# An attention and recurrence kernel on one core: the start of the first batch reordered, and the residual adds of the recurrence put back into its steps

## The chip, the core and the metric

The kernel runs on one core of a Trainium2 chip. The metric is the time of one execution on the device in microseconds (us). A run is the median of several executions; the profile is that of one execution, and times inside it are counted from the start of its span. The engines are PE (TensorE's products; PEld is its weight load), DVE (VectorE), ACT (ScalarE), POOL (GpSimd) and SP (SyncE, which here only issues transfers).

## What is computed

The input x has the shape 4 x 128 x 64 x 64: four batches of 128 channels by 4096 positions. All is in 32-bit floats. Cut to what matters, the reference is:

```python
# layer 0
x = x + conv_attention(groupnorm(x, 32 groups))      # q, k: 64 x 128 weights, v: 128 x 128
                                                     # softmax over all 4096 positions
# layer 1, on tokens t = x transposed to (4, 4096, 128)
t = t + causal_attention(layernorm(t), Wq, Wk, Wv)   # scale 128 ** -0.5
t = t + ffn(layernorm(t), W, V, gamma, beta)
# the ffn
Wx = batchnorm(einsum('bti,hi->bth', t, W)) * gamma + beta   # over all batches and tokens
y = 0
for each token: y = sigmoid(Wx[token] + y @ V.T)             # 4096 steps, every y is an output
```

## The kernel before

**Storage.** `X` (128 partitions x 4 batches x 4096) stays in SBUF from the first load to the end. It is loaded by eight DMAs of 1 MB on SP's queue (L88 to L91). The weights and biases come by 17 DMAs on ACT's queue (L95, L104 to L107), W0k and W0q twice each, since q and k of 64 channels are laid on both halves of the partitions.

**Order of the work.** A scheduler sets the order of the instructions on each engine by the order in which the program makes them and by what they need; `keep_in_program_order` holds an instruction at its place in the program. The program itself lists units: a tile is (layer, batch, c) with 512 queries, a unit is two blocks of 128 keys. The loop at L496 makes the scores of unit i + 1 (L428), lets up to two queued jobs take a step (`turn`, L225), and then makes the product of unit i (L457). ACT takes the exponential of the scores with a shift (L441), DVE adds the exponentials up for the softmax's sums (L475). A job is a Python generator, such as `groupnorm`, `feed0` (keys and values of 512 positions), `prep0` (queries), `norm1` (layernorm), `end` (division by the sums) or `wx` (the ffn's first product); `complete` runs one to its end on the spot.

**Start of a batch.** `groupnorm` takes bn_stats of X in eight pieces (L260), aggregates them to mv (L264), takes the means of a group by a product (pg L267, copied to gmv L269), the spread of the means by another (dev L271 and L272, pd L275), the inverse root on DVE and POOL (L154, L155), scales the three weights by it (wk, wv, wq, L284), and folds the means into the biases (pb L288, L293). For batch 0 nothing else is there to be done meanwhile; `start_batch(0)` and `score(0)` (L494, L495) run all of it, then the keys and values of eight columns (pk L308, pv L313), the queries of the first tile (pq L319), and a sample of scores (`sample`, pz L238, maximum L242, pm L245, L247, px L250) from which the exponential's shift comes (L252). For layer 1 the product of Wq and Wk is made once ahead of everything (`wt`, pa, A1; L207 to L216); it needs W1q and W1k. `groupnorm` of batches 1 to 3 is queued by `start_batch` in layer 1 of the batch before (L480).

**The recurrence** (`chunks`, L518). The 4096 steps of a batch are cut into 256 chunks of 16 steps that run side by side; each chunk is warmed up by 12 steps of the chunk before. So there are 28 steps, s = -12 to 15, of four batches each: a product with FV on PE (pg L552, 128 x 256), then L554 on DVE (gain times Wx, added to it in PSUM), then the sigmoid on ACT (L555). From s = 0 on each result is added to the layer's input T, which was written to D in DRAM by L379 and loaded back by L193. For batches 0 and 1 POOL adds it in each step (L558, with a stride of 16 in T). For batches 2 and 3 the results are kept in `later`, and DVE adds them behind the last step in eight adds of 128 x 1024 (L567). `out` leaves by DMAs of 2 MB for batches 0 and 1 (L561) and of 1 MB for the other two (L573).

**The flag.** Behind the adds DVE compares the warm-up's last state with the neighbouring chunk's (d L578, L580, L581) and looks at the range of the softmax's sums with two reductions of 128 x 1024 (L587, L588). A product adds the verdicts up (pb L591) into a flag (L594); all engines load it and branch (L603, L604). With these inputs it is zero, and the slower second version, `whole`, is jumped over.

Of the kernel before, what the change touches and what calls it, by code (L numbers as in the profile page):

```python
# [37 lines left out]
L = 16  # L38
M = 4096 // L
LEAD = 12  # L40
# [24 lines left out]
def fast(  # L65
# [10 lines left out]
    nc = tc.nc  # L76
    B, C, N = x.shape
    CQ = w0q.shape[1]
    NQ = N // QT
# [4 lines left out]
    const = ctx.enter_context(tc.tile_pool(name="const", bufs=1))  # L84
    xpool = ctx.enter_context(tc.tile_pool(name="xres", bufs=1))

    X = xpool.tile([P, B, N], F32, name="X")
    for b in range(B):  # L88
        for h in range(2):
            cols = ts(h, N // 2)  # L90
            nc.sync.dma_start(out=X[:, b, cols], in_=x[b, :, cols])  # L91

    def load(src, shape, name):
        t = const.tile(shape, F32, name=name)
        nc.scalar.dma_start(out=t, in_=src)  # L95
        return t


    W0q = const.tile([P, 2, CQ], F32, name="W0q")
    W0k = const.tile([P, 2, CQ], F32, name="W0k")  # L100
    B0q = const.tile([P, 1], F32, name="B0q")
    B0k = const.tile([P, 1], F32, name="B0k")
    for h in range(2):
        nc.scalar.dma_start(out=W0k[:, h, :], in_=w0k)  # L104
        nc.scalar.dma_start(out=W0q[:, h, :], in_=w0q)
        nc.scalar.dma_start(out=B0k[ds(h * CQ, CQ), :], in_=b0k)
        nc.scalar.dma_start(out=B0q[ds(h * CQ, CQ), :], in_=b0q)  # L107
    W0v = load(w0v, [P, C], "W0v")
# [7 lines left out]
    Fbeta = load(fbeta, [P, 1], "Fbeta")  # L116


    ident = const.tile([P, P], F32, name="ident")
# [3 lines left out]
    ones = const.tile([P, P], F32, name="ones")  # L123
    nc.gpsimd.memset(ones, 1.0)
# [23 lines left out]
    gain = const.tile([P, 1], F32, name="gain")  # L148
# [46 lines left out]
    with ExitStack() as actx:  # L195
# [11 lines left out]
        wt = {}  # L207
        for n, w in (("q", W1q), ("k", W1k)):
            pw = ps_m.tile([P, P], F32, tag="m", name=f"pw_{n}")
            nc.tensor.transpose(pw, w, ident)  # L210
            wt[n] = tmp.tile([P, P], F32, tag="wt", name=f"wt_{n}")
            nc.vector.tensor_copy(wt[n], pw)
        pa = ps_m.tile([P, P], F32, tag="m", name="pa")
        nc.tensor.matmul(pa, lhsT=wt["q"], rhs=wt["k"], start=True, stop=True)
        A1 = const.tile([P, P], F32, name="A1")
        nc.vector.tensor_scalar(A1, pa, float(C) ** -0.5, None, ALU.mult)  # L216

        jobs = deque()

# [36 lines left out]
        def groupnorm(b):  # L256

            stats = small.tile([P, NQ, 6], F32, tag="stats", name=f"stats_{b}")
            for c in range(NQ):
                nc.vector.bn_stats(stats[:, c, :], X[:, b, ts(c, QT)])  # L260
                if c % 2:
                    yield
            mv = small.tile([P, 2], F32, tag="mv", name=f"mv_{b}")
# [6 lines left out]
            dev = small.tile([P, 1], F32, tag="dev", name=f"dev_{b}")  # L270
            nc.vector.tensor_tensor(dev, mv[:, 0:1], gmv[:, 0:1], ALU.subtract)  # L271
            nc.vector.tensor_tensor(dev, dev, dev, ALU.mult)  # L272
            yield
            pd = ps_m.tile([P, 1], F32, tag="m", name=f"pd_{b}")
            nc.tensor.matmul(pd, lhsT=gmat, rhs=dev, start=True, stop=True)  # L275
            nc.vector.tensor_tensor(gmv[:, 1:2], pd, gmv[:, 1:2], ALU.add)
            grs = small.tile([P, 1], F32, tag="grs", name=f"grs_{b}")
            rsqrt(grs, gmv[:, 1:2], 1e-5, 1)
            yield
            got = {}  # L280
            for n, w in (("k", W0k), ("v", W0v), ("q", W0q)):
                src = w if n == "v" else w.rearrange("p h o -> p (h o)")
                got[n] = small.tile([P, P], F32, tag=f"w{n}", name=f"w{n}_{b}")
                nc.vector.tensor_scalar(got[n], src, grs, None, ALU.mult)  # L284
# [123 lines left out]
        def score(i):  # L408
# [16 lines left out]
            ps = ps_pair.tile([P, 2, QT], F32, tag="pair", name=f"ps_{i}")  # L425
            for h in range(2):
                rows = slice(0, P) if layer else ds(h * CQ, CQ)
                nc.tensor.matmul(  # L428
                    ps[:, h, first[h] :], lhsT=K[layer, b][rows, ts(2 * u + h, P)],
                    rhs=Q[t][rows, first[h] :], start=True, stop=True,  # L430
                )
            if layer and u >= 2 * c:
# [85 lines left out]
def chunks(tc, X, T, gain, bias, FV, ones, sums, out, flag):  # L518
# [4 lines left out]
    with ExitStack() as ctx:  # L523
        yp = ctx.enter_context(tc.tile_pool(name="ys", bufs=5))
        keep = ctx.enter_context(tc.tile_pool(name="keep", bufs=1))
        ps_g = ctx.enter_context(tc.tile_pool(name="ps_g", bufs=1, space=PSUM))


        half = B // 2
        later = keep.tile([P, B - half, L, M], F32, name="later")  # L530
        WX = X.rearrange("p b (c s m) -> p b c s m", s=L, c=X.shape[2] // QT)

        lead = keep.tile([P, B, M + 1], F32, name="lead")
        nc.vector.memset(lead[:, :, 0:1], 0.0)
        last = None
        for s in range(-LEAD, L):
            if s == -1:
                Y = [lead[:, b, 1:] for b in range(B)]
            else:
                y = yp.tile([P, half if s >= 0 else B, M], F32, tag="Y", name=f"Y_{s + LEAD}")  # L540
                Y = [
                    later[:, b - half, s, :] if s >= 0 and b >= half else y[:, b, :] for b in range(B)
                ]
            for b in range(B):
                wx = WX[:, b, :, s % L, :]
                if last is None:
                    nc.scalar.activation(  # L547
                        Y[b].rearrange("p (c m) -> p c m", c=wx.shape[1]), wx, AF.Sigmoid, bias=bias, scale=gain
                    )
                    continue  # L550
                ps = ps_g.tile([P, M], F32, tag=f"g{b}", name=f"pg_{s + LEAD}_{b}")
                nc.tensor.matmul(ps, lhsT=FV, rhs=last[b], start=True, stop=True)  # L552
                pv = ps.rearrange("p (c m) -> p c m", c=wx.shape[1])
                nc.vector.scalar_tensor_tensor(pv, wx, gain, pv, ALU.mult, ALU.add)  # L554
                nc.scalar.activation(Y[b], ps, AF.Sigmoid, bias=bias)  # L555
                if s >= 0 and b < half:
                    t = T[b].rearrange("p (m s) -> p s m", s=L)[:, s, :]
                    nc.gpsimd.tensor_tensor(t, t, Y[b], ALU.add)  # L558
            last = [lead[:, b, :M] for b in range(B)] if s == -1 else Y
        for b in range(half):  # L560
            nc.sync.dma_start(out=out[b], in_=T[b])  # L561
        for b in range(half, B):
            t = T[b].rearrange("p (m s) -> p s m", s=L)
            for i in range(4):
                cols = ts(i, M // 4)
                tc.keep_in_program_order(
                    nc.vector.tensor_tensor(  # L567
                        t[:, :, cols], t[:, :, cols], later[:, b - half, :, cols], ALU.add
                    )
                )  # L570
                if i % 2:
                    cols = ts(i // 2, M * L // 2)
                    nc.sync.dma_start(out=out[b][:, cols], in_=T[b][:, cols])  # L573
        good = keep.tile([P, 4], F32, name="good")
        d = keep.tile([P, B, M - 1], F32, name="d")
        for b in range(B):
            tc.keep_in_program_order(
                nc.vector.tensor_tensor(d[:, b, :], lead[:, b, 1:M], last[b][:, : M - 1], ALU.subtract)  # L578
            )
# [490 lines left out]
```

## Time and profile before

| | |
|---|---|
| median of 5 runs | 2673.69 us (2672.82 to 2675.09) |
| the profiled execution | 2675.83 us |
| its span | 2674.3 us, mean granted clock 0.99 |
| DMA | 35.81 MB: HBM read 17.30 MB, written 16.78 MB |

The profile of this execution lists: the busy time of each engine; the span in slices, with the clock that PE was granted; the DMA queues; the chain of waits that ended last, followed back from the last instruction; the costliest groups of instructions; and the DMA issues with their time to landing. The trace behind it gives the same for any stretch of time or line. The stages are seen in these moments: the first load is issued at 0.80, the first exponential starts at 49.99, the last tile of attention ends its products at about 2571, the first sigmoid of the recurrence starts at 2593.02, the step s = 0 at 2616.30, the last step ends at about 2645.5, the last of `out` lands at 2666.89.

### The profile page before, as it was taken

What the parts mean: (1) busy time and instruction counts of PE and PEld (TensorE: products, weight loads), DVE (VectorE), ACT (ScalarE), POOL (GpSimd) and SP (SyncE); (2) the same over time, 40 slices, a digit from 0 to 9 for tenths busy, and PEclk for the clock granted to TensorE, in tenths of its full rate; (3) what the DMA queues carried; (4) which work ended last, traced back from release to release, by engine and by line L of the source; (5) the groups of instructions that cost most, each with busy time, mean ns of one, the idle gap of its engine ahead of it and who ended that gap; (6) DMA issues with size and microseconds to landing.
All of it is one profiled execution on the core that took longest, in us unless ns stands there. A gap on an engine that the chain in (4) does not pass through costs nothing.

```text
span 2674.3 us, 25646 instructions
## 1 busy us (share of the span) xinstructions
PE 2598.0 (97%) x9970; PEld 1223.4 (46%) x9970; DVE 1498.7 (56%) x2543; ACT 1118.9 (42%) x1302; POOL 100.2 (4%) x118
## 2 busy tenths in 40 slices
PE   6999999999999999999999999999999999999975
PEld 3444444445444444454444444444544444444443
DVE  4565556544555556554455555654455565655448
ACT  2444443333444444343444444333344444433345
POOL 0000000000000000000000000000000000000004
PEclk9999999999999999999999999999999999999988
DMA  3000000000000000000000000000000000100013
GB/s 134 1 1 1 1 0 11 9 5 4 5 1 1 1 1 5 12 4 5 8 1 1 1 1 1 8 12 4 5 4 1 1 1 1 67 13 4 8 67 127
DMA packets 9522, 35.81 MB, mean 13 GB/s; under 512 B 2224, under 2 KB 2992, under 8 KB 7088
## 3 DMA queue, kind: packets, MB, share of 16 engines
q1 hardware_dynamic: 7200, 33.56, 3.2%
q8 instruction: 80, 1.31, 0.2%
q10 hardware_dynamic: 2192, 0.53, 0.1%
q14 instruction: 50, 0.41, 0.1%
HBM read 17.30 MB, written 16.78 MB: 13 GB/s over the span
## 4 chain that ended last, share of the span: by engine, by line
PE 91%; DVE 6%; ACT 1%; issue 1%; DMA 1%; POOL 0%; ACTq 0%; DVEq 0%; POOLq 0%
PE av L457 47%; PE ps L428 32%; PE pg L552 2%; DVE tot L475 2%; PE pq L319 1%; ACT s L441 1%; PE pv L313 1%; PE pk L308 1%; PE po L377 1%; PE pq L340 1%; PE pw L389 1%; DVE zt L354 1%; DVE tot L351 1%; DVE part L356 1%; PE pt L161 1%
## 5 line engine op out<-in xcount | busy, mean ns | idle before, releaser
L457 PE MATMUL av<-s,V 64*128 64x512 f32 (+3 forms) x4864 | 1361.4, 587 | 0.0
L441 ACT ACTIVATE s<-ps,shift 128x1024 f32<-128x1024 f32 (+4 forms) x796 | 809.2, 1024 | 1317.5 <-PE ps L428 1177.3
L475 DVE TENSOR_TENSOR tot<-tot,s 128x1024 f32<-128x1024 f32 (+4 forms) x796 | 878.8, 1109 | 857.4 <-ACT s L441 732.9
L428 PE MATMUL ps<-q,K 64*128 64x512 f32 (+4 forms) x3200 | 1030.3, 579 | 0.0
L457 PEld LDWEIGHTS av<-s,V 64*128 64x128 f32 (+1 forms) x4864 | 546.0, 187 | 593.4 <-issue 585.9
L428 PEld LDWEIGHTS ps<-q,K 64*128 64x128 f32 (+1 forms) x3200 | 416.5, 188 | 483.4 <-issue 472.1
L457 PE MATMUL av<-tot,V 64*128 64x512 f32 (+2 forms) x384 | 124.6, 612 | 5.8 <-DVE acc L469 5.8
L441 ACT ACTIVATE tot<-ps,shift 128x1024 f32<-128x1024 f32 (+2 forms) x68 | 71.5, 1058 | 104.7 <-PE ps L428 84.0
L155 POOL TENSOR_TENSOR rstd<-rstd,mhalf 128x4 f32<-128x4 f32 x32 | 32.3, 1008 | 1443.8 <-DVE rstd L154 1443.8
L457 PEld LDWEIGHTS av<-tot,V 64*128 64x128 f32 (+1 forms) x384 | 49.5, 190 | 70.5 <-issue 39.1
L155 POOL TENSOR_TENSOR rstd_f<-rstd_f,mhalf 128x4 f32<-128x4 f32 x32 | 33.5, 1046 | 914.4 <-DVE rstd_f L154 914.4
L435 DVE TENSOR_TENSOR ps<-ps,mask 128x128 f32<-128x128 f32 x128 | 38.0, 297 | 33.8 <-PE ps L428 31.5
L174 DVE TENSOR_SCALAR V<-xt,mv,rstd 128x128 f32<-128x128 f32 x128 | 36.0, 342 | 34.5 <-POOL rstd L155 34.5
L174 DVE TENSOR_SCALAR rows<-xt_f,mv_f,rstd_f 128x128 f32<-128x128 f32 x128 | 36.7, 342 | 31.2 <-POOL rstd_f L155 31.2
L554 DVE SCALAR_TENSOR_TENSOR pg<-X,gain,pg 128x256 f32<-128x256 f32 x108 | 48.4, 489 | 5.4 <-PE pg L552 4.7
L354 DVE STREAM_TRANSPOSE zt<-tot 128x512 f32<-128x512 f32 x64 | 45.5, 710 | 2.1
L378 DVE TENSOR_TENSOR X<-X,po 128x512 f32<-128x512 f32 x32 | 22.0, 687 | 43.8 <-PE po L377 43.8
L351 DVE TENSOR_TENSOR tot<-tot 128x512 f32<-128x512 f32 x64 | 44.3, 692 | 2.2
L365 DVE STREAM_TRANSPOSE rt<-sums 128x512 f32<-128x512 f32 x64 | 45.1, 704 | 0.6
L356 DVE TENSOR_REDUCE part<-zt 128x16 f32<-128x512 f32 x64 | 43.9, 686 | 2.1
L552 PE MATMUL pg<-Y,FV 128*128 128x256 f32 x148 | 38.8, 411 | 6.5 <-ACT Y L547 6.5
L363 DVE RECIPROCAL sums<-pz 128x16 f32<-128x16 f32 x64 | 16.4, 257 | 46.7 <-PE pz L361 46.7
(131 smaller groups left out, 1157.2 us busy)
## 6 DMA issues: line engine op xcount, KB each, us to landing
X<-in_x SPq DMA_DIRECT2D x8, 1024.0 KB, 7.6
D<-X SPq DMA_DIRECT2D x32, 256.0 KB, 2.0
T<-D SPq DMA_DIRECT2D x4, 2048.0 KB, 7.8
out<-T SPq DMA_DIRECT2D x2, 2048.0 KB, 7.5
out<-T SPq DMA_DIRECT2D x4, 1024.0 KB, 7.9
W0k<-in_w0k ACTq DMA_DIRECT2D x2, 32.0 KB, 5.0
W0q<-in_w0q ACTq DMA_DIRECT2D x2, 32.0 KB, 4.7
W0v<-in_w0v ACTq DMA_DIRECT2D x1, 64.0 KB, 5.3
```

Of the source, the lines that this page charges most:

```text
L155: nc.gpsimd.tensor_tensor(dst, dst, mhalf[:, :n], ALU.pow)
L174: nc.vector.tensor_scalar(rows[:, j, :], xt[:, j, :], mv[:, j, 0:1], rstd[:, j : j + 1], ALU.subtract, ALU.mult)
L351: nc.vector.tensor_tensor(both, both, total[:, 1, :], ALU.add)
L354: nc.vector.transpose(zt.rearrange("p j a -> p (j a)"), both)
L356: nc.vector.tensor_reduce(part, zt, AX.X, ALU.add)
L365: nc.vector.transpose(rt.rearrange("p (j a) -> p j a", a=R), r.unsqueeze(2).to_broadcast([P, QT // R, R]))
L428: nc.tensor.matmul(ps[:, h, first[h] :], lhsT=K[layer, b][rows, ts(2 * u + h, P)], rhs=Q[t][rows, first[h] :], start=True, stop=True,)
L441: nc.scalar.activation(s[:, *a], ps[:, *a], AF.Exp, bias=shift[layer, b])
L457: nc.tensor.matmul(acc[:, first[h] :], lhsT=V[layer, b][rows, 2 * u + h, :], rhs=s[rows, h, first[h] :], start=u == 0 and h == 0, stop=u = ...
L475: nc.vector.tensor_tensor(total[:, *a], total[:, *a], s[:, *a], ALU.add)
L552: nc.tensor.matmul(ps, lhsT=FV, rhs=last[b], start=True, stop=True)
L554: nc.vector.scalar_tensor_tensor(pv, wx, gain, pv, ALU.mult, ALU.add)
```

## The change

The change rewrites two places.

At the start, X of batch 0 is loaded first, in four pieces of 512 KB on SP's queue; W0k, W0v and W0q come once each on ACT's queue, and all other small loads go to SP's queue behind batch 0, with X of the other batches (2 MB each) last. The weights that were loaded twice are read twice instead. PE multiplies a matrix of ones with itself five times at the start (`busy`), once between pg and pd, and once between pd and pb, for batch 0 only; nothing reads the results. The keys and values of the eight columns are now made one column after another with one step of `prep0` (queries, then the three steps of the sample) behind each, and from the fourth column on a step of `fold` (the product of Wq and Wk). The bn_stats of batches 1 to 3 and the first scores are kept in program order.

In the recurrence, all four batches' results are added in each step: on DVE where s is 3, 7, 11, 14 or 15, on POOL in the other steps. `later` is gone, `out` leaves by one 2 MB transfer per batch behind the last step, d is one subtraction of 128 x 1020 in place of four, and the two reductions over the sums are no longer kept in program order; in the order that the scheduler makes they stand on DVE in the end of the last tile of attention.

```diff
-    for b in range(B):
-        for h in range(2):
-            cols = ts(h, N // 2)
-            nc.sync.dma_start(out=X[:, b, cols], in_=x[b, :, cols])
...
+    for h in range(4):
+        nc.sync.dma_start(out=X[:, 0, ts(h, N // 4)], in_=x[0, :, ts(h, N // 4)])
+    W0k = const.tile([P, CQ], F32, name="W0k")
...
+    for t, src in ((W0k, w0k), (W0v, w0v), (W0q, w0q)):
         nc.scalar.dma_start(out=t, in_=src)
...
+    for b in range(1, B):
+        nc.sync.dma_start(out=X[:, b, :], in_=x[b])
...
+        def busy(n):
+
+            for k in range(n):
+                pw = ps_m.tile([P, 4, P], F32, tag="m", name=f"busy_{k}")
+                nc.tensor.matmul(
+                    pw, lhsT=ones, rhs=ones.unsqueeze(1).to_broadcast([P, 4, P]), start=True, stop=True
+                )
+
+        busy(5)
...
-                nc.vector.bn_stats(stats[:, c, :], X[:, b, ts(c, QT)])
+                st = nc.vector.bn_stats(stats[:, c, :], X[:, b, ts(c, QT)])
+                if b:
+                    tc.keep_in_program_order(st)
...
             nc.vector.tensor_tensor(dev, dev, dev, ALU.mult)
+            if b == 0:
+                busy(1)
             yield
...
             rsqrt(grs, gmv[:, 1:2], 1e-5, 1)
+            if b == 0:
+                busy(1)
             yield
...
         start_batch(0)
+        feeds[0][0].complete()
+        folded = Job(fold())
+        for c in range(NQ):
+            feeds[0][c + 1].complete()
+            preps[0, 0, 0].step()
+            if c > 2:
+                folded.step()
         score(0)
...
-                if s >= 0 and b < half:
+                if s >= 0:
                     t = T[b].rearrange("p (m s) -> p s m", s=L)[:, s, :]
-                    nc.gpsimd.tensor_tensor(t, t, Y[b], ALU.add)
-            last = [lead[:, b, :M] for b in range(B)] if s == -1 else Y
-        for b in range(half):
+                    eng = nc.vector if s >= L - 2 or s % 4 == 3 else nc.gpsimd
+                    eng.tensor_tensor(t, t, y, ALU.add)
+            last = lead[:, :, :M] if s == -1 else Y
+        for b in range(B):
             nc.sync.dma_start(out=out[b], in_=T[b])
-        for b in range(half, B):
-            t = T[b].rearrange("p (m s) -> p s m", s=L)
-            for i in range(4):
-                cols = ts(i, M // 4)
-                tc.keep_in_program_order(
-                    nc.vector.tensor_tensor(
-                        t[:, :, cols], t[:, :, cols], later[:, b - half, :, cols], ALU.add
-                    )
-                )
...
-            tc.keep_in_program_order(nc.vector.tensor_reduce(good[:n, i : i + 1], sums, AX.X, red))
+            nc.vector.tensor_reduce(good[:n, i : i + 1], sums, AX.X, red)
```

In the changed kernel the recurrence's product, DVE instruction and sigmoid are L575, L577 and L578, its adds L582, the products of ones L211.

More of the change, by code (lines that the diff above doesn't have):

```diff
@@ L87, in fast @@
     X = xpool.tile([P, B, N], F32, name="X")
-    for b in range(B):
-        for h in range(2):
-            cols = ts(h, N // 2)
-            nc.sync.dma_start(out=X[:, b, cols], in_=x[b, :, cols])
     def load(src, shape, name):
         t = const.tile(shape, F32, name=name)
+        nc.sync.dma_start(out=t, in_=src)
+        return t
+    for h in range(4):
+        nc.sync.dma_start(out=X[:, 0, ts(h, N // 4)], in_=x[0, :, ts(h, N // 4)])
+    W0k = const.tile([P, CQ], F32, name="W0k")
+    W0v = const.tile([P, C], F32, name="W0v")
+    W0q = const.tile([P, CQ], F32, name="W0q")
+    for t, src in ((W0k, w0k), (W0v, w0v), (W0q, w0q)):
         nc.scalar.dma_start(out=t, in_=src)
-        return t
-    W0q = const.tile([P, 2, CQ], F32, name="W0q")
-    W0k = const.tile([P, 2, CQ], F32, name="W0k")
     B0q = const.tile([P, 1], F32, name="B0q")
@@ L103, in fast @@
     for h in range(2):
[L104 to L108, printed above, removed]
+        nc.sync.dma_start(out=B0k[ds(h * CQ, CQ), :], in_=b0k)
+        nc.sync.dma_start(out=B0q[ds(h * CQ, CQ), :], in_=b0q)
     B0v = load(b0v.rearrange("o c -> c o"), [P, 1], "B0v")
@@ L116, in fast @@
     Fbeta = load(fbeta, [P, 1], "Fbeta")
+    for b in range(1, B):
+        nc.sync.dma_start(out=X[:, b, :], in_=x[b])
+    ones = const.tile([P, P], F32, name="ones")
+    nc.gpsimd.memset(ones, 1.0)
     ident = const.tile([P, P], F32, name="ident")
@@ L122, in fast @@
     nc.vector.tensor_reduce(same, ident.rearrange("p (i r) -> p r i", r=R), AX.X, ALU.add)
-    ones = const.tile([P, P], F32, name="ones")
-    nc.gpsimd.memset(ones, 1.0)
     mhalf = const.tile([P, 4], F32, name="mhalf")
@@ L204, in fast, with fold @@
         ps_m = actx.enter_context(tc.tile_pool(name="ps_m", bufs=2, space=PSUM))
[L207 to L214, printed above, removed]
-        A1 = const.tile([P, P], F32, name="A1")
-        nc.vector.tensor_scalar(A1, pa, float(C) ** -0.5, None, ALU.mult)
+        def busy(n):
[5 more added lines that the diff above has]
+        busy(5)
+        A1 = const.tile([P, P], F32, name="A1")
+        def fold():
+            wt = {}
+            for n, w in (("q", W1q), ("k", W1k)):
+                pw = ps_m.tile([P, P], F32, tag="m", name=f"pw_{n}")
+                nc.tensor.transpose(pw, w, ident)
+                wt[n] = tmp.tile([P, P], F32, tag="wt", name=f"wt_{n}")
+                nc.vector.tensor_copy(wt[n], pw)
+            yield
+            pa = ps_m.tile([P, P], F32, tag="m", name="pa")
+            nc.tensor.matmul(pa, lhsT=wt["q"], rhs=wt["k"], start=True, stop=True)
+            nc.vector.tensor_scalar(A1, pa, float(C) ** -0.5, None, ALU.mult)
+            yield
         jobs = deque()
@@ L281, in groupnorm @@
             for n, w in (("k", W0k), ("v", W0v), ("q", W0q)):
-                src = w if n == "v" else w.rearrange("p h o -> p (h o)")
                 got[n] = small.tile([P, P], F32, tag=f"w{n}", name=f"w{n}_{b}")
-                nc.vector.tensor_scalar(got[n], src, grs, None, ALU.mult)
+                dst = got[n]
+                if n != "v":
+                    dst = dst.rearrange("p (h o) -> p h o", h=2)
+                    w = w.unsqueeze(1).to_broadcast([P, 2, CQ])
+                nc.vector.tensor_scalar(dst, w, grs, None, ALU.mult)
             yield
@@ L427, in score @@
                 rows = slice(0, P) if layer else ds(h * CQ, CQ)
-                nc.tensor.matmul(
+                mm = nc.tensor.matmul(
                     ps[:, h, first[h] :], lhsT=K[layer, b][rows, ts(2 * u + h, P)],
@@ L431, in score @@
                 )
+                if i == 0:
+                    tc.keep_in_program_order(mm)
             if layer and u >= 2 * c:
@@ L526, in chunks @@
         ps_g = ctx.enter_context(tc.tile_pool(name="ps_g", bufs=1, space=PSUM))
-        half = B // 2
-        later = keep.tile([P, B - half, L, M], F32, name="later")
         WX = X.rearrange("p b (c s m) -> p b c s m", s=L, c=X.shape[2] // QT)
@@ L536, in chunks @@
         for s in range(-LEAD, L):
[L537 to L543, printed above, removed]
+            Y = lead[:, :, 1:] if s == -1 else yp.tile([P, B, M], F32, tag="Y", name=f"Y_{s + LEAD}")
             for b in range(B):
                 wx = WX[:, b, :, s % L, :]
+                y = Y[:, b, :]
                 if last is None:
                     nc.scalar.activation(
-                        Y[b].rearrange("p (c m) -> p c m", c=wx.shape[1]), wx, AF.Sigmoid, bias=bias, scale=gain
+                        y.rearrange("p (c m) -> p c m", c=wx.shape[1]), wx, AF.Sigmoid, bias=bias, scale=gain
                     )
@@ L551, in chunks @@
                 ps = ps_g.tile([P, M], F32, tag=f"g{b}", name=f"pg_{s + LEAD}_{b}")
-                nc.tensor.matmul(ps, lhsT=FV, rhs=last[b], start=True, stop=True)
+                nc.tensor.matmul(ps, lhsT=FV, rhs=last[:, b, :], start=True, stop=True)
                 pv = ps.rearrange("p (c m) -> p c m", c=wx.shape[1])
                 nc.vector.scalar_tensor_tensor(pv, wx, gain, pv, ALU.mult, ALU.add)
-                nc.scalar.activation(Y[b], ps, AF.Sigmoid, bias=bias)
-                if s >= 0 and b < half:
+                nc.scalar.activation(y, ps, AF.Sigmoid, bias=bias)
+                if s >= 0:
                     t = T[b].rearrange("p (m s) -> p s m", s=L)[:, s, :]
-                    nc.gpsimd.tensor_tensor(t, t, Y[b], ALU.add)
-            last = [lead[:, b, :M] for b in range(B)] if s == -1 else Y
-        for b in range(half):
+                    eng = nc.vector if s >= L - 2 or s % 4 == 3 else nc.gpsimd
+                    eng.tensor_tensor(t, t, y, ALU.add)
+            last = lead[:, :, :M] if s == -1 else Y
+        for b in range(B):
             nc.sync.dma_start(out=out[b], in_=T[b])
-        for b in range(half, B):
-            t = T[b].rearrange("p (m s) -> p s m", s=L)
-            for i in range(4):
-                cols = ts(i, M // 4)
-                tc.keep_in_program_order(
-                    nc.vector.tensor_tensor(
-                        t[:, :, cols], t[:, :, cols], later[:, b - half, :, cols], ALU.add
-                    )
-                )
-                if i % 2:
-                    cols = ts(i // 2, M * L // 2)
-                    nc.sync.dma_start(out=out[b][:, cols], in_=T[b][:, cols])
-        good = keep.tile([P, 4], F32, name="good")
[L575 to L579, printed above, removed]
+        good = keep.tile([P, 4], F32, name="good")
+        d = yp.tile([P, B, M - 1], F32, tag="Y", name="d")
+        nc.vector.tensor_tensor(d, lead[:, :, 1:M], last[:, :, : M - 1], ALU.subtract)
         nc.vector.tensor_reduce(good[:, 0:1], d, AX.XY, ALU.max, apply_absolute_value=True)
```

## The prediction

> **What bounds the kernel now.** I read the page first, then the chain of waits from 0 to 60 and from 2500 on, then windows by stage, and last the recurrence instruction by instruction. Times are us from the start of the span of the profiled execution.
>
> ```profile
> PE 2598.0 (97%) x9970; PEld 1223.4 (46%) x9970; DVE 1498.7 (56%) x2543; ACT 1118.9 (42%) x1302; POOL 100.2 (4%) x118
> 80.00:2500.00 2420.00, 2410.74 (x9323) 1120.54 (x9320) 1352.05 (x2272) 1015.67 (x1127) 66.20 (x69) 1.00 0.02 6
> 2616.00:2646.00 30.00, 28.95 (x128) 20.56 (x126) 29.21 (x66) 28.46 (x66) 26.30 (x32) 1.00 0.00 1
> ```
>
> In the second and third line the columns are window, length, then busy time of PE, PEld, DVE, ACT, POOL, the granted clock, the DMA share and GB/s. From 80 to 2500 PE has 2410.7 of 2420 busy: nothing can be gained there, only lost. The change works on the two ends: the start, where PE waits, and the recurrence, where DVE has 29.2 of 30 and nothing to spare. The chain through the start (start, duration, what):
>
> ```profile
> 0.80 5.49 DMA X<-in_x
> ...
> 7.98 7.98 DMA W1q<-in_w1q
> ...
> 16.10 0.46 PE pw_q L210
> ...
> 16.58 0.29 DVE wt_q L212
> ...
> 19.70 0.38 DVE mv L264
> ...
> 24.00 0.30 DVE wk L284
> ...
> 49.25 0.51 PE px L250 x2
> ```
>
> The reader is to see that the statistics of batch 0 don't end on X: they stand behind the copy of `wt_q` (L212), in DVE's order, and that waits for W1q until 15.96. The projections follow wk, and the sample of scores stands alone behind them. The recurrence's adds (min/median/max in ns):
>
> ```profile
> L558 POOL TENSOR_TENSOR T<-T,Y x32: 852/862/2538, 2617.4 to 2645.6; 128x256 f32<-128x256 f32 x32
> L567 DVE TENSOR_TENSOR T<-T,later x8: 1865/1872/2519, 2645.6 to 2658.8; 128x1024 f32<-128x1024 f32 x8
> ```
>
> The two maxima are neighbours: the L558 add of 2645.63 took 2.54 beside an L567 add that began at 2645.59, and the next L567 (2647.42 to 2649.94) took 2.52 and not 1.87. An add of two operands in SBUF on one engine waited for the other's to end. That row decides what the change costs.
>
> **The change, part by part.** All against the profiled execution of 2675.83 (span 2674.3 and 1.5 around it); it is 2.1 above the median of 2673.69, so the sum is taken off the median.
>
> *Start.* SP now issues X of batch 0 first, in four pieces, without a wait for W0k (5.3 on L91 before) or W1q (7.9). A 2 MB load alone took 7.8 (T from D); from 0.80, with 0.13 MB of weights at some 420 GB/s beside it (+0.3), the last piece lands at 8.9. Two bn_stats of 0.62 pitch follow: mv at 10.2, not 19.70: -9.5. From mv to wk it was 4.30, with two bn_stats of batch 1 on the chain (0.60 each), which are gone (-1.2); the two products of ones ahead of pd and pb are two records each, 0.86 at full clock, against gaps of about 0.6 that they fill: +0.5. From wk to the first exponential it was 25.99. Now, at full clock: wk and step 0.4, pb 0.9, eight columns at the steady 1.90 (1.01 pk + 0.89 pv) 15.2, pq 1.03, pz 0.86, pm and px 0.5, the fold's three 0.8, ps 0.86, step 0.1: 20.65, so -5.3; the reductions of the sample (0.69 and 0.28 on DVE) lie beside later columns. Then the half clock:
>
> ```profile
> core 0: us, PE busy (x) PEld busy (x) DVE busy (x) ACT busy (x) POOL busy (x), PEclk, DMA share, GB/s
> ...
> 46.00:55.30 9.30, 9.30 (x23) 3.73 (x23) 1.13 (x3) 2.23 (x2) 0.00 (x0) 0.63 0.00 0
> ```
>
> PE waited for the sample in the us before, and the records show 0.5 from 48.46 to 55.29. From the first exponential (49.99) to the third unit's av (59.82) it took 9.83; at 2.575 a unit it is 1.17 + 2.575 x 2 + 0.86 (pq) = 7.2: -2.6. The 12 small loads and the other batches' 6 MB that follow on SP's queue are wanted late (W1q by the fold some 15 us on, batch 1 at its statistics, hundreds of us on) and cost nothing; ACT is rid of 14 issues. Start in all: **-18.1**. It is -13 if the projections are cold for 7 us as now (24.3 to 31.39, at half clock, 3.57 a column and not 1.90: three columns, +5), and -21 if X's pieces land so that their bn_stats end with them and nothing of the ones shows.
>
> The clock speaks to the products of ones as well: PE began its dense work at 24.34, and the first record at full clock is 31.39, 7 us later. "TensorE: Matmul & The Clock Gate" of the Trainium skill (The HAM clock gate, What's actually happening) gives about 3.4 us of sustained work until the full clock. By the page the five products (some 9 us cold) are more than enough and the sum stands; by the row they are just enough, and the gaps from mv to wk may undo it, which is the -13.
>
> *bn_stats of batches 1 to 3.* Before, 24 of them (0.68 median) lay beside the loads and projections of batch 0. Now, kept in program order, they stand in four pairs per batch between DVE's adds of layer 1 of the batch before. Below: nothing, since DVE has 1352 of 2420 there. Above: all of 24 x 0.68 = 16, which would need every pair on PE's path. Near the diagonal a pair (1.35) can stand ahead of the mask add that an exponential waits for; I take half of one pair per batch: **+2**.
>
> *Reductions of the sums.* L587, 1.14 each at the very end before, stand in the after-order between rt and u and between u and the add into X, in the last tile's end chain (2570.5 to 2593, one chain without slack). The first delays u: **+1.15**. The second lies beside po (2.09). Bounds 0 and +2.3.
>
> *Adds in the steps.* Before: 32 adds on GpSimd beside the steps, the rest after the last step. Now all 64 are in the steps: 44 on GpSimd, 20 on DVE (s = 3, 7, 11, 14, 15). From the first L554 of s = 0 (2616.30) to T of batch 0 ready (2645.71) it took 29.4. Until the last add of batch 0 now, DVE has 62 L554 at pitch 0.4475 (27.75) and 17 adds. Such an add isn't in the trace; a contiguous 128x255 (d, L578) took 0.40 at pitch 0.33, and the strided 128x1024 of L567 1.80 pitch, or 0.45 for a quarter. I take 0.52, as the fixed part is paid more often: 8.8. Twelve of them (s = 3, 7, 11) meet a GpSimd that has fallen behind (an add every 0.81, so 3.2 per step, against a step of 1.79). In the order of the after-kernel three come together and the fourth after three L554: the first and fourth wait half an add (0.4), the others a whole one (0.74): 0.57 on average, 6.8. Behind a waiting add on DVE stand the next L554, and behind these the sigmoids and products of the next step, so each wait is paid in full. Sum 43.4: **+14.0**. GpSimd's own queue agrees: 1.1 + 44 x 0.81 + 12 x 0.52 = 43.0. Bounds: without any waiting for each other GpSimd alone sets it, 1.1 + 35.6 = 36.7: +7.3; each of the 17 a full 1.26 more: 27.75 + 21.4, +20.
>
> *Clock in the steps.* Where DVE does T adds, PE waits: in a step of some 6 us (1.79 + 4 x 1.09) it has 1.71 of work. Before, a gap of under a us in the sample was followed by 6.8 us at half clock. At half clock the first steps had L554 every 0.853 (2594.93, 2595.78, 2596.63), 3.41 a step, 1.62 more. Much of that lies beside GpSimd's backlog (12 adds, 9.7, per four steps). I take **+2**, between 0 and eight steps, +13.
>
> *End.* out is now four 2 MB transfers issued within some 2 us. Before, 8.39 MB took from 2645.71 to 2666.89, 21.2, at 396 GB/s, the queue being the limit: no change. But after the landing came 7.4 to the end of the span, since DVE's eight L567 delayed the flag to 2666.45 and the branch behind it took PE 4.0 (2667.08 to 2671.09). Now d (1.2), a reduction (1.2) and the flag (1.0) end some 4 after the last add, the branch 5 later, all beside the transfer; left are the 3.1 that SP needed after its last wait (2671.21 to 2674.27) and 0.5: **-3.8** (0 to -5). `later`'s 15 us of adds were beside the transfers, so their going gains only this.
>
> Sum: -18.1 + 2 + 1.15 + 14.0 + 2 - 3.8 = **-2.7**, 2673.1 profiled, **2671.0** by the median.
>
> **Rivals.** The measurement can tell about 0.2% (5.3 us) from no change: 2668.3 to 2679.0 counts as the same.
>
> A, the forecast, 2671.0, own range 2666 to 2677: chance 0.45.
>
> B, the adds don't hold each other up as feared: the one collision in the trace is with adds four times as long. Then T is ready at +7.3, the bursts are short, the clock stays: -18.1 + 2 + 1.15 + 7.3 - 3.8 = -11.5, **2662.2**. Against it: both maxima above fit a whole wait. Chance 0.30, and with it goes a start better than reckoned.
>
> C, slower: the half clock. Place: L576's products after each burst of T adds. Price: 1.62 a step. At eight of sixteen steps it is +13 and not +2, **2682**; beyond A it decides from six or seven steps at half clock on. For it: at 77% busy the sample's window sufficed. Against it: at half clock PE is busy throughout, which lifted it again after 4.55 us in the recurrence's beginning (2593.67 to 2598.22). Chance 0.15.
>
> D, the start doesn't come earlier as written: the products of ones run late at half clock (10 records of 1.0 end at 11, ahead of pg in PE's order), the gaps keep it cold, and X's pieces share the queues with 12 small loads and 6 MB behind them (before, a 1 MB load among others took up to 13.1). Start -9 and not -18: **2680**. Chance 0.10.
>
> Faster: 0.28 of B and 0.08 of A: 0.36. Same: 0.35 of A, 0.02 each of B and C, 0.05 of D: 0.44. Slower: 0.13 of C, 0.05 of D, 0.02 of A: 0.20. The range runs from B with 3 more at the start, 2659, to C with 2 more of statistics, 2684.
>
> **What would show it.** In the profile of the changed kernel: mv of batch 0 near 10 and the first exponential near 34, clock 1.0 from there (start; D if later than 40). GpSimd adds of up to 1.3 beside DVE adds of up to 1.2 at s = 3, 7, 11 (A), or both near 0.86 and 0.45 (B). From the first L577 of s = 0 to the first out issue 45 (A), 37 (B), 55 (C, with records at 0.5 in it). No wait of PE over 1 us at the pairs of bn_stats. Flag well before the last landing, and the end within 4 of it. The forecast is wrong if the waits at s = 3, 7, 11 are absent, or if the clock falls for more than a window at each.

## The result and the profile after

The changed kernel takes 2679.0 us (median of 27 runs, 2675.57 to 2681.3) against 2673.66 for the kernel before, measured beside it (47 runs, 2672.16 to 2676.11). The ratio is 1.0017, with a 95% interval of 1.0012 to 1.0023: 5.3 us slower where 2.7 faster was forecast. Its runs fall into two groups, 10 of 27 up to 2677.2 and the others from 2678.0 to 2681.3, with a mean granted clock of 0.989 to 0.990 in the first and 0.987 to 0.989 in the second; the profile is of the first (2676.84, span 2674.8), and a second one below is of the other.

The page of the profile after, by engine (busy time, share of the span, instructions):

```profile
PE 2603.8 (97%) x9984; PEld 1221.9 (46%) x9984; DVE 1498.3 (56%) x2552; ACT 1118.8 (42%) x1302; POOL 111.0 (4%) x130
```

The same by window (window, length, PE, PEld, DVE, ACT, POOL, clock, DMA share, GB/s):

```profile
80.00:2500.00 2420.00, 2409.34 (x9281) 1118.09 (x9278) 1362.10 (x2294) 1012.93 (x1125) 65.69 (x69) 1.00 0.02 6
...
2616.00:2646.00 30.00, 21.20 (x88) 14.34 (x88) 29.59 (x56) 18.90 (x44) 30.00 (x35) 1.00 0.00 1
```

Two things changed. In the steps (last line) DVE is as full as before, but now GpSimd is full too, and PE has fallen from 28.95 to 21.20 of 30: the products wait. (The time that an add spends waiting for the other engine stands in these rows as busy.) In the main stage DVE has 10 us more, and PE 1.4 less busy in the same window. The chain through the start:

```profile
1.71 6.49 DMA X<-in_x
...
8.23 1.29 DVE stats L274 x2
9.52 0.28 DVE same L125
...
10.04 1.21 DVE stats L274 x2
...
11.27 0.38 DVE mv L280
...
14.01 1.88 PE busy L211 x2
15.88 0.34 PE pb L311 x4
...
28.45 1.12 PE pk L331 x2
...
38.07 1.12 ACT tot L466
```

The reader is to see that W1q is gone from the chain and that X now carries it, that two small instructions of DVE (`same` and, behind it, `blocks`) stand among the statistics, that a product of ones is itself on the chain ahead of pb, and that the first exponential starts at 38.07 and not at 49.99.

The adds in the steps, by engine:

```profile
L582 POOL TENSOR_TENSOR T<-T,Y x44: 860/896/1192, 2608.1 to 2646.8; 128x256 f32<-128x256 f32 x44
L582 DVE TENSOR_TENSOR T<-T,Y x20: 566/1182/1354, 2613.6 to 2651.4; 128x256 f32<-128x256 f32 x20
```

DVE's add takes 0.57 at the least and 1.18 in the median; GpSimd's takes up to 1.19.

Stage by stage, from the two profiles, in us against before:

| stage | forecast | measured |
|---|---|---|
| start, to the third unit's av (59.82, now 45.75) | -18.1 | -14.1 |
| layer 1 of batches 0 to 2 (three tiles, 1.18 each) | +2 | +3.55 |
| last tile's end, last `zt` to the first sigmoid (21.14, now 22.05) | +1.15 | +0.9 |
| warm-up steps (23.28, now 23.61) | 0 | +0.3 |
| s = 0 to the first out issue (29.41, now 42.50), clock included | +16.0 | +13.1 |
| first out issue to the end of the span (28.56, now 25.30) | -3.8 | -3.3 |
| sum | -2.7 | +0.5 |

What lies outside the span grew by 0.5 (from 1.5 to 2.0). The rest of the 5.3 is where the profiled executions stand among their runs: the one of before is 2.1 above its median, the one of after 2.2 below its.

### The profile page after: what moved, and what is told of

The parts are those of the page before. It is cut to its first block, busy times and chain, and to the rows that moved or that the text cites. A ratio compares the mean times of both kernels' runs of the same rounds, so it can differ in the third digit from the quotient of the medians.

```text
span 2674.8 us, 25695 instructions
## 1 busy us (share of the span) xinstructions
PE 2603.8 (97%) x9984; PEld 1221.9 (46%) x9984; DVE 1498.3 (56%) x2552; ACT 1118.8 (42%) x1302; POOL 111.0 (4%) x130
## 4 chain that ended last, share of the span: by engine, by line
PE 88%; DVE 9%; ACT 1%; issue 1%; DMA 0%; POOL 0%; SPq 0%; DVEq 0%; POOLq 0%; ACTq 0%
PE av L482 47%; PE ps L451 31%; DVE tot L500 2%; DVE pg L577 1%; PE pq L342 1%; ACT s L466 1%; PE pv L336 1%; PE po L400 1%; PE pk L331 1%; PE pq L363 1%; PE pw L412 1%; DVE zt L377 1%; DVE tot L374 1%; DVE part L379 1%; PE pt L162 1%
## 5 line engine op out<-in xcount | busy, mean ns | idle before, releaser
L575 PE MATMUL pg<-Y,FV 128*128 128x256 f32 x208 | 51.7, 407 | 18.5 <-ACT Y L578 12.0
L578 ACT ACTIVATE Y<-pg,bias 128x256 f32<-128x256 f32 x104 | 45.6, 474 | 18.3 <-DVE pg L577 17.6
L575 PEld LDWEIGHTS pg<-Y,FV 128*128 128x128 f32 x208 | 34.9, 198 | 36.0 <-ACT Y L578 19.0
L577 DVE SCALAR_TENSOR_TENSOR pg<-X,gain,pg 128x256 f32<-128x256 f32 x108 | 47.9, 488 | 5.5 <-PE pg L575 5.1
L401 DVE TENSOR_TENSOR X<-X,po 128x512 f32<-128x512 f32 x32 | 22.0, 688 | 42.5 <-PE po L400 42.5
```

The lines of the kernel that those rows point to most:

```text
L575: nc.tensor.matmul(ps, lhsT=FV, rhs=last[:, b, :], start=True, stop=True)
L578: nc.scalar.activation(y, ps, AF.Sigmoid, bias=bias)
```

## The experiments

The theory after the comparison: the table's stages account for the two spans, the kept bn_stats cost their 3.55 because pg waits for them, the adds cost what two engines that shut each other out must cost, and the second group of runs is a longer stretch at half clock. The rivals are named with each experiment.

**The two halves apart.** `e1_start_only` has all of the change but the recurrence and the end, `e2_steps_only` these alone. The whole function `chunks` is exchanged; here only its head is shown:

```diff
 # e1_start_only: the changed kernel, with the function of the kernel before
-def chunks(...)   # all adds in the steps
+def chunks(...)   # `later` and L567, reductions of the sums kept in program order
 # e2_steps_only: the other way round
```

> The changed kernel's start, weights, ones and kept bn_stats, with the recurrence and the end of the kernel before. Theory, from the two profiles by stage: the start gains 14.1 (third unit's av at 45.75 and not 59.82), the kept bn_stats cost 3 x 1.18 in layer 1, and the rest of the difference lies behind the attention: this kernel is 10.5 faster than before, 2663, and its runs lie within 2 us of each other as those of before do. Rival: the 4 us between the two groups in which the runs of the changed kernel lie (2676 and 2680) arise at the start, where the clock warms up: then this one shows two groups too.

Measured: 2663.47 (2662.47 to 2666.11, 6 runs), ratio to before 0.9956 (0.9941 to 0.997). The mechanism and the size hold. On the groups it is undecided: four runs lie within 1.1 us, the others at 2664.64 and 2666.11.

> The kernel before with the changed recurrence and end (all adds in the steps, reductions of the sums in attention's end). Theory: +13.1 for the adds, +0.9 for the reduction in attention's end, +0.3, and -3.3 behind the adds: 11 slower than before, 2685, in two groups some 4 apart. Rival for the groups: they come from the start, then this kernel has one group.

Measured: 2684.57 (2683.98 to 2687.08, 7 runs), ratio 1.0034 (1.0021 to 1.0046). Between s = 0 and the first out issue its profile has 43.57. On the groups this one is undecided too: five runs lie within 1.1 us, the others at 2686.6 and 2687.08. The two halves, -10.3 and +10.8, give +0.5, the sum of the table, which is of the first group; between the medians it is 5.3. That the missing 4.8 is the second group fits its distance of about 4, but why the halves show it in so few of their runs isn't shown.

**The second group.** The changed kernel once more:

> The changed kernel once more, for a second profile. Its runs lie in two groups, 2675.6 to 2677 at a mean clock of 0.990 and 2679 to 2681 at 0.987; the profile at hand is of the first. Theory: if this one falls in the second, the recurrence has a stretch or two at half clock beside its bursts of adds on DVE. Rival: the stretch lies at the start, between the products of ones and the projections.

It took 2680.93, of the second group. The windows of the start, first of the profile after, then of this one:

```profile
0.00:24.00 24.00, 18.57 (x54) 9.07 (x55) 8.37 (x23) 4.74 (x7) 2.95 (x14) 0.93 0.77 283
```

```profile
0.00:24.00 24.00, 18.76 (x44) 10.04 (x45) 7.67 (x22) 3.66 (x5) 2.94 (x14) 0.79 0.78 290
```

The five products and the wait behind them, in the profile after:

```profile
1.06 6.74 PE L211 MATMUL busy<-ones 128*128 128x512 f32 x10 [1.06 <-POOL ones L121]
...
11.79 0.35 PE L283 MATMUL pg<-mv,group 128*128 128x2 f32 x2 [4.00 <-DVE mv L280]
```

The clock column is the answer: 0.93 against 0.79. It doesn't show the cold beginning: up to 5.5 the records of the ones follow each other every 0.85 us and from there on every 0.43, while the column stands at 1.00, so the beginning is read from the durations. The five products of ones end at 7.8, PE then waits 4.0 for mv (3.8 in the other execution), and the clock falls: in the first execution from 12.3 for 3.4 us, in this one from 12.5 for 10.2, through the first columns. The second tile starts 2.8 later (82.24 against 79.44). Of the 4.1 between the two spans 2.8 lie there, 0.4 in the warm-up steps (one stretch of 3.4 more at half clock) and 0.9 in the adds (two stretches of 3.4). The theory as I had put it, a stretch in the recurrence, holds for the smaller part; the rival, the start, for two thirds. That is one profile of each group; where the other runs lost their time wasn't recorded. The profiles of the kernels below with the same five products widen the picture: the ones reach full clock between 4.5 and 7.1, and the sooner they do, the sooner they end and the longer is the gap. With a gap of 3.2 (e3) the clock didn't fall, with 3.5 (e1) and 4.1 (e6b) it fell for 3.4 us, with 4.5 (e8) and 4.6 (e6) for 6.8.

**The products of ones.** None at all, at the start and in `groupnorm`, and nine in place of five at the start:

```diff
 # e5_no_ones
-        busy(5)
...
-            if b == 0:
-                busy(1)
 # e7_nine_ones
-        busy(5)
+        busy(9)
```

> The changed kernel without any product of ones. Theory: the ones raise the clock before the projections; without them PE is idle until pg, and the first three or four columns run at half clock as they did before (24.3 to 31.4), about 5 us, less the 1 us that the products between pg, pd and pb hold these up: the first exponential comes at 42 and not at 38.1 (first group) or 40.9 (second group), and the kernel is some 2 to 4 slower than the changed one, 2681 to 2683. Rival: the ones are worth nothing, since the gap of 4 us behind the five undoes them: 2679 or less.

Measured: 2679.44 (2678.43 to 2680.65, 11 runs): one group, below the expected 2681 to 2683 and not told apart from the changed kernel's median. Its first column runs cold (the two records of pk at 15.36 take 2.05, against 1.10 in the profile after), and the first exponential came at 41.27, close to the expected 42, so the ones do raise the clock. The changed kernel's median shows nothing of it: the second profile, with its first exponential at about 40.9, had lost it again. The rival is right: five products and two fillers are worth nothing in the median.

> The changed kernel with nine products of ones at the start in place of five. Theory: the five end at 7.8 and the clock falls in the gap until pg at 11.8 (half clock from 12.3 for 3.4 us in one execution, for 10.2 in another, which makes most of the two groups); with nine the product is dense until about 11.2, there is no half clock between 6 and the end of attention, and the runs make one group near the faster end: 2675.5. Rival: the two groups come from the recurrence, and stay.

Measured: 2675.91 (2675.44 to 2677.15, 11 runs). Its start:

```profile
0.00:24.00 24.00, 21.02 (x67) 10.37 (x67) 8.53 (x24) 5.53 (x8) 2.95 (x14) 1.00 0.77 282
```

```profile
1.06 9.72 PE L211 MATMUL busy<-ones 128*128 128x512 f32 x18 [1.06 <-POOL ones L121]
...
11.78 0.35 PE L283 MATMUL pg<-mv,group 128*128 128x2 f32 x2 [1.00 <-DVE mv L280]
```

The gap is 1.0, the clock column is 1.00, the first exponential comes at 37.09, and the runs make one group. The groups are thus mostly a matter of the gap behind the ones; in warm-up and steps the clock may still differ from run to run by the 1.3 that the second profile showed.

**The kept bn_stats.** The changed kernel without the order that keeps them:

```diff
                 st = nc.vector.bn_stats(stats[:, c, :], X[:, b, ts(c, QT)])
-                if b:
-                    tc.keep_in_program_order(st)
```

> The changed kernel, with the bn_stats of batches 1 to 3 free for the scheduler again. Theory: the 1.18 that each batch loses once in layer 1 is the wait of pg and pd for statistics that stand late on DVE; free, they go into the start's idle DVE, and 3.5 of the 3.5 come back: 2675.5 against 2679. Rival: the losses come from the changed place of pg and pd in PE's order; then nothing comes back, and the bn_stats at the start may delay the first batch.

Measured: 2675.5 (2672.64 to 2677.35, 12 runs), as forecast. From the second tile's first exponential to the last tile's it takes 2423.5; the changed kernel takes 2427.1, and the kernel before 2423.6. So the loss is undone to within 0.1, with the jobs queued as in the changed kernel; the scheduler then puts pg of batch 1 a few products earlier, between two whole scores. This is where it was lost in the changed kernel (PE's and DVE's rows of one tile, start, duration):

```profile
502.40 1.02 PE L451 MATMUL ps<-q,K 128*128 128x512 f32 x2
...
502.86 0.55 DVE L500 TENSOR_TENSOR tot<-tot,s 128x384 f32<-128x384 f32 x1
503.33 0.37 DVE L280 BATCH_NORM_AGGREGATE mv<-stats 128x2 f32<-128x48 f32 x1
...
503.75 0.38 PE L283 MATMUL pg<-mv,group 128*128 128x2 f32 x2 [0.33 <-DVE mv L280]
```

The statistics and mv stand behind DVE's work on the diagonal, and pg stands in PE's order between the two halves of a score, so the second half (504.47) waits for it too. A second gap follows ahead of pd (506.49). Against the same products in e3 (498.87 to 508.08) PE starts pg 0.5 late and pd 0.3 late; the rest of the 1.18 is tenths around them.

**The adds: two engines that exclude each other?** In both kernels DVE's 20 adds stand four together behind the step's L577 and take a constant of zeros as the second operand, once from PSUM, once from SBUF. The results that these 20 would add are left out of the output:

```diff
+        pc = ps_g.tile([P, M], F32, tag="pc", name="pc")      # e6b: keep.tile, in SBUF
+        nc.vector.memset(pc, 0.0)
...
-                    eng.tensor_tensor(t, t, y, ALU.add)
+                    if eng is nc.gpsimd:
+                        eng.tensor_tensor(t, t, y, ALU.add)
+            for b in range(B if s >= 0 and (s >= L - 2 or s % 4 == 3) else 0):
+                t = T[b].rearrange("p (m s) -> p s m", s=L)[:, s, :]
+                tc.keep_in_program_order(nc.vector.tensor_tensor(t, t, pc, ALU.add))
```

> The changed kernel, but DVE's 20 adds take their second operand from a constant of zeros in PSUM in place of the step's result (which these steps leave out of the output), four together behind the step's L554. Theory: DVE and GpSimd exclude each other only where both of DVE's inputs lie in SBUF. Here no add waits: DVE adds near 0.55, GpSimd adds 0.86 at most, s = 0 to the first out issue 37 to 38 in place of 42.5, and 5 faster than its counterpart with the constant in SBUF. Rival: the long adds (1.18 median on DVE) come from the stride or from the burst; then the two are the same.

> The counterpart: the same order on DVE, but the constant of zeros in SBUF (these 20 adds are left out of the output likewise). Theory: as in the changed kernel, adds of 1.18 at s = 3, 7, 11 on DVE and up to 1.2 on GpSimd, s = 0 to the first out issue 42 to 44, the time of the changed kernel within 2. Rival: like the one with PSUM.

Measured: 2672.42 (2670.65 to 2675.17, 10 runs) with the constant in PSUM, 2683.32 (2680.13 to 2685.12, 4 runs) in SBUF; ratios to before 0.9996 (0.9987 to 1.0006) and 1.004 (1.0025 to 1.0055). The adds with PSUM, then with SBUF:

```profile
L585 POOL TENSOR_TENSOR T<-T,Y x44: 855/896/977, 2610.5 to 2645.7; 128x256 f32<-128x256 f32 x44
L588 DVE TENSOR_TENSOR T<-T,pc x20: 597/626/669, 2616.4 to 2647.7; 128x256 f32<-128x256 f32 x20
```

```profile
L585 POOL TENSOR_TENSOR T<-T,Y x44: 856/898/1195, 2608.0 to 2648.2; 128x256 f32<-128x256 f32 x44
L588 DVE TENSOR_TENSOR T<-T,pc x20: 572/1062/1259, 2614.0 to 2653.9; 128x256 f32<-128x256 f32 x20
```

Nothing differs but where one operand lies, and no add of DVE takes over 0.67 or of GpSimd over 0.98 when it is PSUM. From s = 0 to the first out issue it is 37.5 and 46.2, against 42.5 in the changed kernel. The exclusion is shown for these adds, and rival B of the prediction is out. The gain was larger than expected (10.9 between the medians and 8.7 in the steps of the two profiles, not 5), and the counterpart was 3.7 slower in the steps than the changed kernel. Why is not shown: its adds on DVE were shorter in the median (1.06, not 1.18), and its steps hold two stretches of 3.4 us at half clock, which the steps of the changed kernel's first profile lack up to 2647.4.

**The sample among the columns.** The changed kernel, with the queries and the sample behind all eight columns:

```diff
             feeds[0][c + 1].complete()
-            preps[0, 0, 0].step()
             if c > 2:
```

> The changed kernel, but the queries of the first tile and the sample of scores come behind all eight columns, as before the change. Theory: among the columns the sample costs PE 2.4 in waits for PSUM that is read late (columns of 2.5 to 3.3 in place of 1.90), behind them it costs its chain and the half clock that follows; the first exponential comes at about 38.3 as now, the third unit's av some 2.6 later, and the kernel is 2 to 3 slower than the changed one: 2681 to 2682. Rival: the waits are a loss that nothing repays, and this kernel is as fast or faster: 2677 to 2679.

Measured: 2680.49 (2678.39 to 2684.99, 9 runs), ratio to before 1.0025 (1.0015 to 1.0035). That interval overlaps the changed kernel's: by the time alone it is inconclusive. Its profile shows the mechanism: waits of 0.8 for q and 0.8 for m, half clock from 38.6 for 6.8 us, the third unit's av at 50.9 and not 45.75. Of these 5.1, 1.4 are there before the first pv (19.11, not 17.68), by the longer half clock behind the ones. In the 3.7 that are left, what the interleaving saves in the sample's chain is larger than what it costs in PSUM waits, at least in this pair of profiles.

**What pays, together.** Start with nine products of ones and free bn_stats, recurrence and end of the kernel before:

> The parts that paid, together: the changed start with nine products of ones and with free bn_stats, the recurrence and end of the kernel before. Theory, by adding the measured parts: 2663.5 for the start alone, -3.5 for the bn_stats (three times 1.18), -1 to -2 for the ones that keep the clock: 2658 to 2659.5, faster than both kernels. Rival: freed bn_stats of batch 1 stand at the start beside the first batch's and hold up mv or the sample; then 2661 or more.

Measured: 2658.67 (2658.17 to 2659.64, 5 runs), ratio to before 0.994 (0.9927 to 0.9954): faster than both kernels. Last, the same with the reductions of the sums free:

```diff
-            tc.keep_in_program_order(nc.vector.tensor_reduce(good[:n, i : i + 1], sums, AX.X, red))
+            nc.vector.tensor_reduce(good[:n, i : i + 1], sums, AX.X, red)
```

> The same with the two reductions of the sums no longer kept in program order; the order has them on DVE around the last bn_stats of attention's end. Theory: the first lies in a gap there, the second holds up the chain to the first sigmoid by 1.1, and behind the recurrence the flag comes 2.3 earlier, which the end follows: 1.1 faster than with them kept, 2657 to 2658.5. Rival: the end follows the landing of out and not the flag; then it is 1.1 slower.

Measured: 2658.85 (2658.16 to 2659.85, 5 runs): no difference from the one before it. Both effects are there and cancel. The first sigmoid is 1.2 later (2579.31, not 2578.12); the flag is only 0.8 earlier (2650.89, not 2651.69), and the end comes 3.6 behind the landing of out (2654.31) where it came 5.6 behind it (2652.16). That fits an end that follows the landing once the flag is early enough, but doesn't show it: in the changed kernel the end came 1.5 behind the landing.

## Why the prediction was wrong

It was wrong by 8.0 and in its direction: forecast A, no change on the faster side, against a measured loss of 5.3, at the bound of 0.2% (5.3 us) that the prediction took for no change.

**Start: the step that failed.** The mechanism was right (X and not W1q on the chain, the sample hidden, no half clock at 48), and e1 shows that the start pays; its size was -14.1 and not -18.1. By its own terms: mv came at 11.27 and not 10.2, because X's pieces landed one by one at 5.32, 6.80, 8.21 and 9.51 (I had the last at 8.9), and `same` and `blocks` stood ahead of the last pair of bn_stats. From wk to the first exponential it was 23.0 and not 20.65: I let the sample's steps cost PE only their own records, while they share two PSUM buffers with the columns. In the profile after, columns with a step of the sample or the fold among them stand 2.5 to 3.5 apart (pk at 16.08, 19.54, 22.62, 25.16, 28.45, 31.14), and only those without at 1.90 (33.05, 34.95). What releases pk is a read of one of these buffers:

```profile
19.51 0.30 PEld L331 LDWEIGHTS pk<-X,wk 128*128 128x128 f32 x2 [0.64 <-ACT V L337]
...
22.62 0.30 PEld L331 LDWEIGHTS pk<-X,wk 128*128 128x128 f32 x2 [0.76 <-ACT V L337]
...
25.16 1.12 PE L331 MATMUL pk<-X,wk 128*128 128x512 f32 x2 [0.37 <-DVE m L261]
```

From the first exponential to the third unit's av it was 7.7 and not 7.2, from mv to wk 3.8 and not 3.6.

**The same step's clock.** I had seen that the gaps from mv to wk might undo the ones, and put it as the end of -13 and into rival D, with a chance of 0.10. It happened in part: in the second group's profile the half clock takes 2.8 more there, for -11.3 at the start, and 17 of 27 runs lie in that group. What I overlooked is the gap ahead of those gaps: five products end at 7.8, 4.0 before pg. I had reckoned them cold throughout (some 9 us, and an end at 11 in rival D); in fact they were at full clock from 5.5 on and so ended sooner, and the clock they had raised was lost by waiting. Nine products closed it (e7). Of the 8.0, then, 4.0 are the start's size and, if the median run is like the second profile, 2.8 its clock. Rival D's 2680 is near the measured 2679.0 by luck in part: its late ones and slow loads were not seen, and the adds were cheaper than in its sum.

The clock-gate rule of the Trainium skill that I weighed says that about 3.4 us of sustained work raises the clock ("TensorE: Matmul & The Clock Gate", The HAM clock gate, What's actually happening), and the same section's table has it fall after an idle window of that length. For the rising the runs show 3.4 to 6.0 us of dense products (first products at 1.06, full clock at 5.5 in the profile after), and 7 in the kernel before, whose first products had waits of 0.4 and 0.5 among them. The falling was the half of the rule that bore on this change, and I used only the first. The falls behind gaps of 3.5 us and more agree with it; the one at 48.46 in the kernel before and the one at 38.6 in e8 came behind waits of under 1 us each, which the rule as I cite it doesn't cover.

**bn_stats.** Mechanism right (e3), size 3.55 and not 2: I had DVE's mask adds in mind, while it is pg itself that PE waits for, once per batch, at 1.18.

**Reductions.** +0.9 against +1.15: right. e10 shows the price of one at another place of the same chain, 1.2.

**Adds.** +13.1 against +14.0 and +2 for the clock. Right in mechanism, by the strongest test here (e6 against e6b), and close in size: a wait of 0.61 in the median (1.18 less 0.57) where I had 0.57. In the first group's profile the clock fell only at 2647.4, two us before the first out issue, and in the second's, with two stretches of 3.4 us at half clock, the adds took 0.9 longer. So rival C, at eight steps, is out, and the +2 was more than was seen.

**End.** -3.3 against -3.8: right. The flag is done at 2655.1, 18.2 ahead of the last landing (2673.29); before it was 0.4 ahead.

**Against the base.** The stage table compares two single executions. The one after lies in the first group and 2.2 below its median, and the one before 2.1 above its own, so the table shows 0.5 of a loss of 5.3; for a kernel whose clock differs from run to run one profile doesn't stand for the median.

## What to carry to other kernels

Work that only keeps the clock up is worth its place only if it lasts until the real work starts: count when it ends at the clock that it reaches, not at the one it starts from. Adds like these, with all operands in SBUF, one on VectorE and one on GpSimd, are to be counted as one resource: while one runs the other waits. Here an operand of VectorE's add in PSUM took the wait away. Small steps that are slipped between products can cost more than their own records when they share the products' PSUM buffers, and a product that waits for a late statistic stops all that is queued behind it.

## What the runs showed of the hardware

The granted clock's stretches at half come in multiples of about 3.4 us: 3.4, 6.8, 10.2, 23.9 and 27.3 in these profiles. After gaps of 3.5 to 4.6 us it was at half for one to three of these, and not in the order of the gap (10.2 us behind 3.8, 3.4 behind 4.0); after a gap of 3.2 it stayed at full clock. After waits of 0.8 and 0.8 in e8 it was at half for two. The exclusion of DVE and GpSimd works both ways: 0.57 became up to 1.35 on DVE, 0.86 up to 1.19 on GpSimd, and L577, whose second tensor is in PSUM, stayed at 0.46 to 0.51 beside them.
